# A graph-convolution layer with residual and layer norm: the norm moves into the residual's tile, row groups are formed two at a time from the fifth superrow, and the gather ring starts uncleared

## The chip, the cores and the metric

The kernel runs on one core of one Trainium2 chip. The metric is the device time of one execution in microseconds (us). TensorE is called PE here, VectorE DVE, ScalarE ACT, GpSimd POOL and SyncE SP; PEld is the loading of weights into PE.

## What is computed

Sizes: B = 8 batches, N = 4096 nodes, 256 features in and out, all float32. About two in a thousand entries of `adj` are set before it is made symmetric, with a heavy head: low node numbers have many neighbours.

```python
HW = einsum('bnf,fo->bno', x, W)
A_norm = relu((A + A.T) * 0.5)
D = sum(A_norm, axis=1)
d = where(D > 0, D ** -0.5, 0)
L = eye(N) - d[:, None] * A_norm * d[None, :]
y = relu(einsum('nm,bmo->bno', L, HW))
out = layernorm(x + y)            # over the last axis, eps 1e-5
```

## The kernel before

**Stage one** reads `adj` in blocks of 512 x 512. For superrow i (eight of them, 512 rows each) and j >= i, `symmetrise` (L310) transposes a block on PE, adds its partner on DVE (L318), takes relu and the half on ACT (L319), sums 64-wide pieces into `part` on DVE (L320), and stores the block to `a_dram` from ACT's queue (L326). `degrees(i)` (L333) follows each superrow: row sums, their power -0.5 on POOL (`r`), and four diagonal blocks stored to `a_dram` over the stored block.

In between, `form(m, known)` (L355) makes row group m of G = x W: 128 nodes with all eight batches, a tile of 128 x 2048. It loads `xin` over SP's queue, transposes it on PE (L364), copies it on ACT (L365), multiplies it on PE (L374), and scales by `r` on ACT (L383) into `gt`, which goes to `g_dram` (L387). Row groups 24 to 31 are formed first, while their `r` isn't known; they stay unscaled in `held`, and `release` (L391) scales and stores them at the end of the stage. A `credit` (L407) decides how many row groups are formed after each block: one for each pair of blocks. Row groups 21 to 23 are left for the end.

From superrow 0 on, POOL, PE and DVE also make lists of the 64-wide pieces of A that are not empty: `patterns`, `place`, `spread`, `index` and so on. The lists of a unit give the rows to be gathered for it.

**Stage two** works by units u (16 of them), each of two row groups of the output, 2u and 2u+1; "group i" below is one of these 32. For a tile t of a unit's list, `gather` (L519) fetches 128 weights' rows from `a_dram` into `ga` (L527), and the matching 128 rows of `g_dram` into one of the 13 tiles of `ring` (L536), both with POOL's indirect DMAs. PE multiplies tile by tile (L623) into eight PSUM banks, four for group 2u (tag b0) and four for 2u+1 (tag b1). A list entry beyond the end has index N, and `bounds_check` decides whether such a row is fetched or left as it was; row N of `g_dram` and `a_dram` is zero. The ring's tiles are set to zero before use (L514).

When a group's last tile is through, `finish` (L558) runs its end:
- `evict`: ACT moves the four banks to `y` with relu and scale (L449, 128 x 512 each).
- one step later `moments`: DVE adds the residual `xr` (L458), takes the statistics (L463, L465, L466). `residual` (L441) then loads the `xr` of group i+2.
- five steps after that `normalise`: POOL's power (L470), DVE's eight scalings (L472), and the store of `y` to `out` over SP's queue (L480).

Before a unit ends, `lists(u)` (L569) makes the lists of later units: a few matmuls into two PSUM banks of tag b0, and DVE's list steps (L155 to L287, and L244 among them), which must have read these banks before PE can write the next unit's b0 group. Pools set the buffers: `y` has three, `xr` two. Nothing else but these buffers, the data and the order on each engine's queue decides when an instruction runs; the order is fixed when the program is built, and each engine takes its instructions in that order.

Of the kernel before, what the change touches and what calls it, by code (L numbers as in the profile page):

```python
# [8 lines left out]
F32 = mybir.dt.float32  # L9
AF = mybir.ActivationFunctionType  # L10
ALU = mybir.AluOpType
# [29 lines left out]
def kernel(  # L41
# [23 lines left out]
    nc = tc.nc  # L65
    B, N, F = x.shape
    FO = w.shape[1]
    P = 128
    S = 512
    A = S // P  # L70
    NS = N // S
    NB = N // P
# [6 lines left out]
    RING = 13  # L79
# [18 lines left out]
    r = const.tile([P, NB], F32, name="r")  # L98
# [194 lines left out]
    with (  # L293
# [8 lines left out]
        def load_adj(i, j):  # L302
            t = apool.tile([P, A, S], F32, tag="adj", name=f"adj_{i}_{j}")
            nc.sync.dma_start(
                t,
                adj[i * S : (i + 1) * S, j * S : (j + 1) * S].rearrange("(a p) s -> p a s", p=P),
            )
            return t
# [44 lines left out]
        held = {}  # L353
# [36 lines left out]

        def release(m):  # L391
            g = held.pop(m)
            nc.scalar.mul(g, g, r[:, m : m + 1])
            nc.scalar.dma_start(g_dram[m * P : (m + 1) * P, :], g)


        known, early = [], list(range(NB - HOLD, NB))
        credit = 0.0
        for i in range(NS):
            diag = stat1.tile([P, A, P], F32, tag="diag", name=f"diag_{i}")  # L400
            for j in range(i, NS):
                tij = load_adj(i, j)
                tji = load_adj(j, i) if j > i else tij
                symmetrise(i, j, tij, tji)
                if j > i:
                    symmetrise(j, i, tji, tij)
                credit += 1.0 if j > i else 0.5  # L407
                while credit >= 1.0 and (known or early):
                    if known:
                        form(known.pop(0), True)  # L410
                    else:
                        form(early.pop(0), False)
                    credit -= 1.0
                credit = min(credit, 1.0)
            degrees(i)
            known += range(i * A, min((i + 1) * A, NB - HOLD))
            if i < 2:
                for u in (2 * i, 2 * i + 1):
                    patterns(u)
                    tot = psum.tile([P, NK * NB], F32, tag="ix", name=f"tot_{u}", bufs=2)  # L420
                    low = psum.tile([P, NK * NB], F32, tag="ix", name=f"low_{u}", bufs=2)
                    count(u, tot, low)
                    place(u, tot, low)
            elif i < 4:
                for u in (2 * i - 4, 2 * i - 3)[: 4 - i]:
                    pr = psum.tile([P, 2, NB], F32, tag="ix", name=f"pr_{u}", bufs=2)
                    count_rest(u, pr[:, 0], pr[:, 1])
                    place_rest(u, pr[:, 0], pr[:, 1])
            elif i < 6:
                u = i - 4  # L430
                spread(u)
                pl = psum.tile([P, 2, tiles[u]], F32, tag="ix", name=f"pl_{u}", bufs=2)
                collect(u, pl)
                index(u, pl)
        for m in sorted(held):
            release(m)
        for m in known:
            form(m, True)


    def residual(i, ypool):  # L441
        xr = ypool.tile([P, B, F], F32, tag="xr", name=f"xr_{i}", bufs=2)
        nc.scalar.dma_start(xr, x[:, i * P : (i + 1) * P, :].rearrange("b p f -> p b f"))
        return xr

    def evict(i, py, ypool):
        y = ypool.tile([P, B, FO], F32, tag="y", name=f"y_{i}", bufs=3)
        for c in range(G // S):
            nc.scalar.activation(  # L449
                y.rearrange("p b o -> p (b o)")[:, c * S : (c + 1) * S],  # L450
                py[c],
                AF.Relu,
                scale=minus_r[:, i : i + 1],
            )
        return y

    def moments(i, y, xr, stat):
        nc.vector.tensor_add(y, y, xr)  # L458
        stats = stat.tile([P, B, 6], F32, tag="stats", name=f"stats_{i}")
        mv = stat.tile([P, B, 2], F32, tag="mv", name=f"mv_{i}")  # L460
        rstd = stat.tile([P, B], F32, tag="rstd", name=f"rstd_{i}")
        for b in range(B):
            nc.vector.bn_stats(stats[:, b, :], y[:, b, :])  # L463
        for b in range(B):
            nc.vector.bn_aggr(mv[:, b, :], stats[:, b, :])  # L465
        nc.vector.tensor_scalar(rstd, mv[:, :, 1], EPS, None, ALU.add)  # L466
        return mv, rstd

    def normalise(i, y, mv, rstd):
        nc.gpsimd.tensor_tensor(rstd, rstd, neg_half[:, :B], ALU.pow)  # L470
        for b in range(B):
            nc.vector.tensor_scalar(  # L472
                y[:, b, :],
                y[:, b, :],
                mv[:, b, 0:1],
                rstd[:, b : b + 1],
                ALU.subtract,
                ALU.mult,
            )
        nc.sync.dma_start(out[:, i * P : (i + 1) * P, :].rearrange("b p f -> p b f"), y)  # L480

    a_rows = a_dram.rearrange("j (c q) -> (j c) q", q=P)
    a_pairs = a_dram.rearrange("j (c q) -> (j c) q", q=2 * P)
# [22 lines left out]
    with (  # L506
# [3 lines left out]
        tc.tile_pool(name="psum2", bufs=4, space=bass.MemoryType.PSUM) as psum,  # L510
    ):
        ring = [gath.tile([P, G], F32, tag=f"g{k}", name=f"g{k}", bufs=1) for k in range(RING)]
        for gt in ring:
            nc.vector.memset(gt, 0.0)  # L514
        steps = [(u, step) for u in range(NU) for step in steps_of(u)]
        order = [(u, k, t) for u, step in steps for k, t in step]
        got = {}
# [1 line left out]
        def gather(n):  # L519

            if n >= len(order):
                return
            u, kind, t = order[n]
            gi, ai = plan[u]
            both = len(targets(kind)) == 2
            at = gath.tile([P, 2 * P], F32, tag="a", name=f"ga_{u}_{t}")
            nc.gpsimd.indirect_dma_start(  # L527
                out=at if both else at[:, :P],
                out_offset=None,
                in_=a_pairs if both else a_rows,  # L530
                in_offset=bass.IndirectOffsetOnAxis(ap=ai[:, t : t + 1], axis=0),
            )


            gt = ring[n % RING]
            nc.gpsimd.indirect_dma_start(  # L536
                out=gt,
                out_offset=None,
                in_=g_dram,
                in_offset=bass.IndirectOffsetOnAxis(ap=gi[:, t : t + 1], axis=0),  # L540
                bounds_check=N - 1,
                oob_is_err=False,
            )
            got[u, t] = (at, gt)
# [3 lines left out]
        def after(n, fn, *args):  # L548
            later.append((n, fn, args))

        for n in range(RING):
            gather(n)
        n = RING
        xr = {i: residual(i, ypool) for i in range(2)}
        py = {}
        left = {}

        def finish(i):  # L558
            y = evict(i, py.pop(i), ypool)

            def rest():
                mv, rstd = moments(i, y, xr.pop(i), stat)
                if i + 2 < NB:
                    xr[i + 2] = residual(i + 2, ypool)
                after(5, normalise, i, y, mv, rstd)

            after(1, rest)

# [86 lines left out]
    with tc.If(short > 0):  # L655
        with (
            tc.tile_pool(name="full", bufs=3) as full,
            tc.tile_pool(name="ypool3", bufs=2) as ypool,
            tc.tile_pool(name="stat3", bufs=3) as stat,
            tc.tile_pool(name="psum3", bufs=8, space=bass.MemoryType.PSUM) as psum,  # L660
        ):
            for i in range(NB):
                lt = full.tile([P, NB, P], F32, tag="l", name=f"l_{i}", bufs=2)
                nc.sync.dma_start(
                    lt, a_dram[:N, i * P : (i + 1) * P].rearrange("(m p) q -> p m q", p=P)
                )
                py = [psum.tile([P, S], F32, tag="ps", name=f"pz_{i}_{c}") for c in range(G // S)]
                for m in range(NB):
                    gt = full.tile([P, G], F32, tag="g", name=f"gf_{i}_{m}", bufs=4)
                    nc.sync.dma_start(gt, g_dram[m * P : (m + 1) * P, :])  # L670
                    for c in range(G // S):
                        nc.tensor.matmul(
                            py[c],
                            lhsT=lt[:, m, :],
                            rhs=gt[:, c * S : (c + 1) * S],
                            start=(m == 0),
                            stop=(m == NB - 1),
                        )
                y = evict(i, py, ypool)
                mv, rstd = moments(i, y, residual(i, ypool), stat)  # L680
                normalise(i, y, mv, rstd)


# [26 lines left out]
```

## Time and profile before

| What | us |
|---|---|
| three runs | 1771.97, 1778.17, 1779.72 |
| median | 1778.17 |
| profiled execution | 1779.99 |
| its span, first to last instruction | 1778.2 |
| PE busy, of the span | 1521.4 (86%) |
| DVE busy | 823.4 (46%) |
| POOL busy | 804.5 (45%) |
| ACT busy | 368.7 (21%) |
| first matmul of stage two, after the start | 587.0 |

The page divides the span into 40 slices of 44 us. Of each it gives the busy tenths, here PE's, then the granted clock, then the share of the 16 DMA engines:

```profile
PE   6998686868866799999999999998979849679874
...
PEclk8999898989987899999999999999999979889988
DMA  9999999999977984797999999899998986877973
```

Stage one fills the first 13 slices and is full of DMA traffic; stage two begins in the 14th. A busy PE isn't PE at its peak, since matmuls overlap and their ends are modelled. Idle time of an engine that isn't the bottleneck costs nothing.

### The profile page before, as it was taken

What the parts mean: (1) busy time and instruction counts of PE and PEld (TensorE: products, weight loads), DVE (VectorE), ACT (ScalarE), POOL (GpSimd) and SP (SyncE); (2) the same over time, 40 slices, a digit from 0 to 9 for tenths busy, and PEclk for the clock granted to TensorE, in tenths of its full rate; (3) what the DMA queues carried; (4) which work ended last, traced back from release to release, by engine and by line L of the source; (5) the groups of instructions that cost most, each with busy time, mean ns of one, the idle gap of its engine ahead of it and who ended that gap; (6) DMA issues with size and microseconds to landing.
All of it is one profiled execution on the core that took longest, in us unless ns stands there. A gap on an engine that the chain in (4) does not pass through costs nothing.

```text
span 1778.2 us, 18495 instructions
## 1 busy us (share of the span) xinstructions
PE 1521.4 (86%) x6504; PEld 804.2 (45%) x6504; DVE 823.4 (46%) x1841; ACT 368.7 (21%) x457; POOL 804.5 (45%) x1079
## 2 busy tenths in 40 slices
PE   6998686868866799999999999998979849679874
PEld 5887575757755244343433333333333314224331
DVE  5686898656644000425154264346344245233134
ACT  3555443535545000101011001001000100000011
POOL 3000000000003453566767777678677764575641
PEclk8999898989987899999999999999999979889988
DMA  9999999999977984797999999899998986877973
GB/s 338 387 376 376 403 342 348 347 375 392 396 262 281 406 329 152 261 362 266 398 366 387 375 360 372 330 361 357 353 376 305 379 326 214 326 270 284 354 284 112
DMA packets 234547, 590.67 MB, mean 332 GB/s; under 512 B 19863, under 2 KB 122567, under 8 KB 194839
## 3 DMA queue, kind: packets, MB, share of 16 engines
q0 software_dynamic: 57456, 318.57, 46.5%
q1 hardware_dynamic: 100352, 134.23, 21.4%
q10 hardware_dynamic: 76640, 136.61, 20.7%
q8 instruction: 54, 0.88, 0.2%
q14 instruction: 45, 0.37, 0.1%
HBM read 494.47 MB, written 136.34 MB: 355 GB/s over the span
## 4 chain that ended last, share of the span: by engine, by line
PE 54%; DMA 19%; issue 12%; DVE 9%; ACT 3%; POOL 2%; ACTq 0%; POOLq 0%; SPq 0%; DVEq 0%
PE py L623 43%; DMA out_dram<-y 7%; PE pg L374 6%; DMA g<-g_dram,gi 5%; DMA adj<-in_adj_dram 5%; PE tr L315 3%; DVE sym L318 2%; DVE y L472 1%; DVE g L514 1%; ACT sym L319 1%; DVE part L320 1%; ACT xt L365 1%; POOL g L536 1%; POOL ga L527 1%; PE xtr L364 1%
## 5 line engine op out<-in xcount | busy, mean ns | idle before, releaser
L623 PE MATMUL py<-g,ga 128*64 128x512 f32 (+1 forms) x3368 | 1058.3, 601 | 108.8 <-ACT y L449 82.4
L623 PEld LDWEIGHTS py<-g,ga 128*64 128x64 f32 (+1 forms) x3368 | 400.7, 157 | 754.0 <-issue 647.4
L536 POOL DMA_INDIRECT g<-g_dram,gi x317 | 385.2, 1215 | 295.3 <-PE py L623 176.2
L527 POOL DMA_INDIRECT ga<-a_dram,ai x317 | 336.2, 1060 | 131.4 <-issue 84.9
L458 DVE TENSOR_TENSOR y<-y,xr 128x2048 f32<-128x2048 f32 x32 | 73.3, 2290 | 640.4 <-ACT y L449 640.4
L449 ACT ACTIVATE y<-py,minus_r 128x512 f32<-128x512 f32 x128 | 83.5, 688 | 1104.9 <-PE py L623 639.9
L374 PE MATMUL pg<-w_sb,xt 128*128 128x256 f32 x1024 | 253.9, 405 | 63.2 <-ACT xt L365 63.1
L374 PEld LDWEIGHTS pg<-w_sb,xt 128*128 128x128 f32 x1024 | 203.0, 203 | 107.2 <-ACT xt L365 77.8
L318 DVE TENSOR_TENSOR sym<-tr,adj 128x512 f32<-128x512 f32 x256 | 159.3, 683 | 125.3 <-PE tr L315 100.9
L340 POOL TENSOR_TENSOR r<-e,neg_half 128x4 f32<-128x4 f32 x8 | 8.1, 1012 | 402.4 <-DVE e L339 402.4
L315 PE MATMUL tr<-ident,adj 128*128 128x128 f32 x1024 | 132.3, 288 | 43.4 <-DMA adj<-in_adj_dram 26.7
L320 DVE TENSOR_REDUCE part<-sym 128x32 f32<-128x2048 f32 x64 | 144.2, 2277 | 19.6 <-ACT sym L319 19.6
L319 ACT ACTIVATE sym<-sym 128x2048 f32<-128x2048 f32 x64 | 122.4, 1912 | 142.6 <-DVE sym L318 104.7
L315 PEld LDWEIGHTS tr<-ident,adj 128*128 128x128 f32 x1024 | 123.1, 150 | 52.8 <-issue 23.1
L472 DVE TENSOR_SCALAR y<-y,mv,rstd 128x256 f32<-128x256 f32 x256 | 86.9, 412 | 89.3 <-POOL rstd L470 89.3
L463 DVE BATCH_NORM_STATS2 stats<-y 128x6 f32<-128x256 f32 x256 | 86.9, 410 | 0.6
L383 ACT ACTIVATE gt<-pg,r 128x512 f32<-128x512 f32 x96 | 66.0, 690 | 99.7 <-PE pg L374 77.4
L470 POOL TENSOR_TENSOR rstd<-rstd,neg_half 128x8 f32<-128x8 f32 x32 | 53.5, 1673 | 48.0 <-DVE rstd L466 47.3
L364 PE MATMUL xtr<-ident,xin 128*128 128x128 f32 x512 | 67.3, 283 | 9.0 <-ACT gt L383 6.0
L365 ACT COPY xt<-xtr 128x512 f32<-128x512 f32 x128 | 68.9, 582 | 15.6 <-PE xtr L364 9.1
L244 DVE TENSOR_TENSOR hot<-iota_q,at 128x4096 bf16<-128x4096 f32 x16 | 70.6, 4415 | 0.0
L364 PEld LDWEIGHTS xtr<-ident,xin 128*128 128x128 f32 x512 | 59.9, 146 | 13.1 <-ACT gt L383 6.8
(92 smaller groups left out, 380.6 us busy)
## 6 DMA issues: line engine op xcount, KB each, us to landing
adj<-in_adj_dram SPq DMA_DIRECT2D x64, 1024.0 KB, 11.9
a_dram<-sym ACTq DMA_DIRECT2D x64, 1024.0 KB, 10.0
xin<-in_x_dram SPq DMA_DIRECT2D x32, 1024.0 KB, 15.6
xr<-in_x_dram ACTq DMA_DIRECT2D x32, 1024.0 KB, 15.4
out_dram<-y SPq DMA_DIRECT2D x32, 1024.0 KB, 18.8
g_dram<-gt ACTq DMA_DIRECT2D x24, 1024.0 KB, 7.2
g_dram<-held ACTq DMA_DIRECT2D x8, 1024.0 KB, 9.1
ga<-a_dram,ai POOLq DMA_INDIRECT x317, 8.0
```

The costliest lines, as they stand in the source:

```text
L315: nc.tensor.transpose(pt[:, c * P : (c + 1) * P], tji[:, c, a * P : (a + 1) * P], ident)
L318: nc.vector.tensor_add(sym[:, a, :], pt, tij[:, a, :])
L319: nc.scalar.activation(sym, sym, AF.Relu, scale=0.5)
L320: nc.vector.tensor_reduce(part[:, i * A : (i + 1) * A, j * S // Q : (j + 1) * S // Q], sym.rearrange("p a (c q) -> p a c q", q=Q), AX.X, A ...
L364: nc.tensor.transpose(pt[:, k, c, :], xin[:, b + k, c * P : (c + 1) * P], ident)
L365: nc.scalar.copy(xt[:, b : b + 2], pt)
L374: nc.tensor.matmul(pg[:, k * FO : (k + 1) * FO], lhsT=xt[:, b + k, c, :], rhs=w_sb[:, c, :], start=(c == 0), stop=(c == FC - 1),)
L463: nc.vector.bn_stats(stats[:, b, :], y[:, b, :])
L472: nc.vector.tensor_scalar(y[:, b, :], y[:, b, :], mv[:, b, 0:1], rstd[:, b : b + 1], ALU.subtract, ALU.mult,)
L527: nc.gpsimd.indirect_dma_start(out=at if both else at[:, :P], out_offset=None, in_=a_pairs if both else a_rows, in_offset=bass.IndirectOff ...
L536: nc.gpsimd.indirect_dma_start(out=gt, out_offset=None, in_=g_dram, in_offset=bass.IndirectOffsetOnAxis(ap=gi[:, t : t + 1], axis=0), boun ...
L623: nc.tensor.matmul(py[2 * u + b][c][rows, :], lhsT=at[:, off + rows.start : off + rows.stop], rhs=gt[:, c * S : (c + 1) * S], start=new_ro ...
```

## The change

- The addition's result is written into the residual's tile, called `z` in the new code. Statistics, scaling and the store work on it. `y` holds the evicted group only until the addition has read it. `xr` gets three buffers in place of two, `y` two in place of three.
- The load of the residual goes over SP's queue, not ACT's. It is issued for group i+3 after the store of group i, and no longer for i+2 after the addition of i. Since it takes the tile that group i leaves, it waits for that store.
- From superrow 4 on (the fifth), the credit of a block is doubled, so that two row groups may be formed after a pair.
- Held row groups are released after the superrow that they belong to: 24 to 27 after superrow 6, 28 to 31 after superrow 7. Of these the odd ones are scaled on DVE.
- The ring is not set to zero. The first 13 gathers fetch the zero row N for entries beyond the end, in place of leaving the tile as it is.

```diff
@@ -390,8 +390,12 @@
         def release(m):
             g = held.pop(m)
-            nc.scalar.mul(g, g, r[:, m : m + 1])
+            if m % 2:
+                nc.vector.tensor_scalar(g, g, r[:, m : m + 1], None, ALU.mult)
+            else:
+                nc.scalar.mul(g, g, r[:, m : m + 1])
             nc.scalar.dma_start(g_dram[m * P : (m + 1) * P, :], g)
+
         known, early = [], list(range(NB - HOLD, NB))
@@ -404,7 +408,7 @@
                 symmetrise(i, j, tij, tji)
                 if j > i:
                     symmetrise(j, i, tji, tij)
-                credit += 1.0 if j > i else 0.5
+                credit += (1.0 if j > i else 0.5) * (1 if i < 4 else 2)
                 while credit >= 1.0 and (known or early):
                     if known:
                         form(known.pop(0), True)
@@ -413,6 +417,9 @@
                     credit -= 1.0
                 credit = min(credit, 1.0)
             degrees(i)
+            for m in range(i * A, (i + 1) * A):
+                if m in held:
+                    release(m)
             known += range(i * A, min((i + 1) * A, NB - HOLD))
             if i < 2:
                 for u in (2 * i, 2 * i + 1):
@@ -432,19 +439,17 @@
                 pl = psum.tile([P, 2, tiles[u]], F32, tag="ix", name=f"pl_{u}", bufs=2)
                 collect(u, pl)
                 index(u, pl)
-        for m in sorted(held):
-            release(m)
         for m in known:
             form(m, True)
     def residual(i, ypool):
-        xr = ypool.tile([P, B, F], F32, tag="xr", name=f"xr_{i}", bufs=2)
-        nc.scalar.dma_start(xr, x[:, i * P : (i + 1) * P, :].rearrange("b p f -> p b f"))
+        xr = ypool.tile([P, B, F], F32, tag="xr", name=f"xr_{i}", bufs=3)
+        nc.sync.dma_start(xr, x[:, i * P : (i + 1) * P, :].rearrange("b p f -> p b f"))
         return xr
     def evict(i, py, ypool):
-        y = ypool.tile([P, B, FO], F32, tag="y", name=f"y_{i}", bufs=3)
+        y = ypool.tile([P, B, FO], F32, tag="y", name=f"y_{i}", bufs=2)
         for c in range(G // S):
             nc.scalar.activation(
                 y.rearrange("p b o -> p (b o)")[:, c * S : (c + 1) * S],
@@ -454,30 +459,31 @@
             )
         return y
-    def moments(i, y, xr, stat):
-        nc.vector.tensor_add(y, y, xr)
+    def moments(i, y, z, stat):
+
+        nc.vector.tensor_add(z, z, y)
         stats = stat.tile([P, B, 6], F32, tag="stats", name=f"stats_{i}")
         mv = stat.tile([P, B, 2], F32, tag="mv", name=f"mv_{i}")
         rstd = stat.tile([P, B], F32, tag="rstd", name=f"rstd_{i}")
         for b in range(B):
-            nc.vector.bn_stats(stats[:, b, :], y[:, b, :])
+            nc.vector.bn_stats(stats[:, b, :], z[:, b, :])
         for b in range(B):
             nc.vector.bn_aggr(mv[:, b, :], stats[:, b, :])
         nc.vector.tensor_scalar(rstd, mv[:, :, 1], EPS, None, ALU.add)
         return mv, rstd
-    def normalise(i, y, mv, rstd):
+    def normalise(i, z, mv, rstd):
         nc.gpsimd.tensor_tensor(rstd, rstd, neg_half[:, :B], ALU.pow)
         for b in range(B):
             nc.vector.tensor_scalar(
-                y[:, b, :],
-                y[:, b, :],
+                z[:, b, :],
+                z[:, b, :],
                 mv[:, b, 0:1],
                 rstd[:, b : b + 1],
                 ALU.subtract,
                 ALU.mult,
             )
-        nc.sync.dma_start(out[:, i * P : (i + 1) * P, :].rearrange("b p f -> p b f"), y)
+        nc.sync.dma_start(out[:, i * P : (i + 1) * P, :].rearrange("b p f -> p b f"), z)
     a_rows = a_dram.rearrange("j (c q) -> (j c) q", q=P)
     a_pairs = a_dram.rearrange("j (c q) -> (j c) q", q=2 * P)
@@ -510,8 +516,6 @@
         tc.tile_pool(name="psum2", bufs=4, space=bass.MemoryType.PSUM) as psum,
     ):
         ring = [gath.tile([P, G], F32, tag=f"g{k}", name=f"g{k}", bufs=1) for k in range(RING)]
-        for gt in ring:
-            nc.vector.memset(gt, 0.0)
         steps = [(u, step) for u in range(NU) for step in steps_of(u)]
         order = [(u, k, t) for u, step in steps for k, t in step]
         got = {}
@@ -538,7 +542,7 @@
                 out_offset=None,
                 in_=g_dram,
                 in_offset=bass.IndirectOffsetOnAxis(ap=gi[:, t : t + 1], axis=0),
-                bounds_check=N - 1,
+                bounds_check=N if n < RING else N - 1,
                 oob_is_err=False,
             )
             got[u, t] = (at, gt)
@@ -551,7 +555,7 @@
         for n in range(RING):
             gather(n)
         n = RING
-        xr = {i: residual(i, ypool) for i in range(2)}
+        xr = {i: residual(i, ypool) for i in range(3)}
         py = {}
         left = {}
@@ -559,10 +563,15 @@
             y = evict(i, py.pop(i), ypool)
             def rest():
-                mv, rstd = moments(i, y, xr.pop(i), stat)
-                if i + 2 < NB:
-                    xr[i + 2] = residual(i + 2, ypool)
-                after(5, normalise, i, y, mv, rstd)
+                z = xr.pop(i)
+                mv, rstd = moments(i, y, z, stat)
+
+                def end():
+                    normalise(i, z, mv, rstd)
+                    if i + 3 < NB:
+                        xr[i + 3] = residual(i + 3, ypool)
+
+                after(5, end)
             after(1, rest)
@@ -677,8 +686,9 @@
                             stop=(m == NB - 1),
                         )
                 y = evict(i, py, ypool)
-                mv, rstd = moments(i, y, residual(i, ypool), stat)
-                normalise(i, y, mv, rstd)
+                z = residual(i, ypool)
+                mv, rstd = moments(i, y, z, stat)
+                normalise(i, z, mv, rstd)
 # ---- launch: one core; inputs and outputs as the reference has them ----
```

## The prediction

> **What bounds the kernel now.** I read the chain that ended last, then the engines' busy time by stage, then the waits of the second stage, then one turn of the repeating pattern in the timeline, and last the transfers' landing times. The chain first, from the page:
>
> ```profile
> PE 54%; DMA 19%; issue 12%; DVE 9%; ACT 3%; POOL 2%; ACTq 0%; POOLq 0%; SPq 0%; DVEq 0%
> PE py L623 43%; DMA out_dram<-y 7%; PE pg L374 6%; DMA g<-g_dram,gi 5%; DMA adj<-in_adj_dram 5%; PE tr L315 3%; DVE sym L318 2%; DVE y L472 1%; DVE g L514 1%; ACT sym L319 1%; DVE part L320 1%; ACT xt L365 1%; POOL g L536 1%; POOL ga L527 1%; PE xtr L364 1%
> ```
>
> The output transfers stand on it with 7%: a store that nobody should need to wait for. Busy time by stage (us; PE, PEld, DVE, ACT, POOL, then clock, DMA share, GB/s):
>
> ```profile
> 900.00:1300.00 400.00, 391.38 (x1587) 146.44 (x1583) 190.50 (x563) 31.91 (x48) 302.30 (x253) 0.99 0.97 362
> 1300.00:1450.00 150.00, 123.47 (x463) 46.86 (x461) 57.86 (x170) 9.91 (x16) 113.47 (x99) 0.93 0.95 358
> 1450.00:1600.00 150.00, 108.01 (x391) 43.56 (x392) 54.31 (x160) 11.43 (x18) 81.70 (x68) 0.85 0.73 268
> ```
>
> Up to 1300 PE is fed; after it both PE and DMA have holes. Who makes the holes, in the waits from 600 on (engine, line, waited for: total us, times, longest):
>
> ```profile
> ACT y L449 <- DMA out_dram<-y: 438.2, 15, 43.1
> ...
> PE py L623 <- ACT y L449: 82.4, 7, 23.6
> ```
>
> Evictions wait for stores of three groups earlier (three y buffers), and PE waits for the evictions. One turn in the timeline (start, duration):
>
> ```profile
> 1387.44 2.42 ACT L449 ACTIVATE y<-py,minus_r 128x512 f32<-128x512 f32 x4 [34.60 <-DMA out_dram<-y]
> ...
> 1389.89 2.29 DVE L458 TENSOR_TENSOR y<-y,xr 128x2048 f32<-128x2048 f32 x1 [13.81 <-ACT y L449]
> 1392.10 2.67 DVE L472 TENSOR_SCALAR y<-y,mv,rstd 128x256 f32<-128x256 f32 x8
> ...
> 1394.83 0.37 SPq L480 DMA_DIRECT2D out_dram<-y  x1
> ...
> 1418.11 2.42 ACT L449 ACTIVATE y<-py,minus_r 128x512 f32<-128x512 f32 x4 [28.25 <-DMA out_dram<-y]
> ...
> 1420.56 2.29 DVE L458 TENSOR_TENSOR y<-y,xr 128x2048 f32<-128x2048 f32 x1 [22.43 <-ACT y L449]
> ...
> 1432.75 4.42 DVE L244 TENSOR_TENSOR hot<-iota_q,at 128x4096 bf16<-128x4096 f32 x1
> ...
> 1438.26 2.75 DVE L472 TENSOR_SCALAR y<-y,mv,rstd 128x256 f32<-128x256 f32 x8
> ```
>
> This is a loop: evict 19, add 19, normalise 17, store 17 lands after 23 us, evict 20, add 20, list work, normalise 18 (done at 1441.0), and so on. DVE takes its instructions in order, and normalise i stands behind add i+2. From add 12 (1148.2) to add 26 (1628.7) a pair of groups takes 480.5 / 7 = 68.6 us.
>
> What a 1 MB transfer takes to land, in 900 to 1300 (last column, median us):
>
> ```profile
> xr<-in_x_dram ACTq DMA_DIRECT2D x12, 1024.0 KB, 20.6
> out_dram<-y SPq DMA_DIRECT2D x11, 1024.0 KB, 19.9
> ```
>
> and in 1300 to 1778:
>
> ```profile
> out_dram<-y SPq DMA_DIRECT2D x17, 1024.0 KB, 17.1
> xr<-in_x_dram ACTq DMA_DIRECT2D x13, 1024.0 KB, 7.5
> ```
>
> A lone one takes about 6 (the last store: 5.1): the rest is the gathers' traffic.
>
> **What the Trainium skill says.** "DMA: Bandwidth & Descriptors", section "Queues, rings and completion order": each DMA engine goes round its queues packet by packet. The landings of 5.1 to 25.1 us for equal stores agree. The same page, "Issuing engines are not separate DMA queues": all issuers end on the same 16 engines, so another issuer saves only issue time; here that is 0.37 us. The same page, "Two DMAs through the same engine are not ordered": a dependent transfer needs its issuer to wait for the first one's semaphore. Hence SP must sit until a store has landed before it may reload that tile; the kernel before has no such pair, so its trace cannot show it. "Perfetto Trace Analysis", "Identifying the Most-Contended Engine": busy matmul time is a poor measure, which is why I go by waits.
>
> **The second stage, part by part.** The group's life moves from y (three buffers) into z, the residual's tile (also three). Evictions now wait only for the addition of two groups earlier: the 438 us of ACT's wait and PE's 82 go. What is late next is the addition. z of group i is reloaded only after store i-3 has landed, so the path is: normalise i-3, store, land, load, land, add i. Before, the load started right after add i-2 and was there in time. The load is thus moved from beside the loop into the loop.
>
> Where does this bind? In the trace of before, the time from issuing store i-3 to add i is 36 us for i=9, 34 (10), 15 (11), 32 (12), 20 (13), 37 (14), 10 (15), 32 (16). The new path needs 19.9 + 20.6 + 0.4 = 41. So it binds from about group 10.
>
> What queues behind the wait: SP now alternates store i, load i+3 (waits for store i), store i+1. In the instruction order of the two builds DVE is nearly the same in this stage, but late normalise 2u and 2u+1 stand together ahead of additions 2u+3 and 2u+4. Behind a waiting add on DVE stand the list steps and the next normalise; the lists of a unit must be read before PE gets two of its four banks for the next unit.
>
> A pair therefore costs: add to the end of the normalise behind the lists, 1420.6 to 1441.0 = 20.4; store 2u; store 2u+1 (SP was held by the wait); load of 2u+4; three issues, 1.2. Load 2u+3 runs beside store 2u+1.
> - Busy rows: 20.4 + 1.2 + 2 x 19.9 + 20.6 = 82.
> - Late rows: 20.4 + 1.2 + 2 x 17.1 + 7.5 = 63.3.
>
> Which holds? Gathers of a late unit are 16 tiles of 1.05 MB and some 0.1 MB of weights, with stores and loads 22 to 23 MB, at 380 GB/s 59 us. They start when PE gets its banks, about 8 us after the add, so the engines are full until some 67 us after it. The first store (22) and the second (19) fall in that time; the last load, at 63, gets the engines nearly alone: 6 to 8. Sum 20.4 + 1.2 + 41 + 8 = 71. I take P = 71, ends 63 and 82.
>
> Start of the loop: stage one ends 8 us earlier (below), so store 7 is issued at 1038.5, lands 1058.4, z of 10 lands 1079.4; add 10 to the end of normalise 8 is 15.1 (1094.5); store 8 to 1114.4; store 9 to 1135; load 12 to 1156. Add 12 is at 1156, before 1148.2. Then seven pairs; the last two units' pairs have no lists, 11 us less each, and the seventh 2 less; from add 30 to add 31 pass 8.5 (statistics and normalise 28), a store of 12 and a load of 8, with issues 29; add 31 to the end as before, 17.5 (1760.7 to 1778.2). Span = 1156 + 7P - 2 + 2(P - 11) + 29 + 17.5 = 1178.5 + 9P. With 71: 1817.5. Break-even is P = 66.6.
>
> **The first stage.** Chain there (start, duration):
>
> ```profile
> 543.38 10.21 DMA g_dram<-held
> ...
> 579.86 1.78 DVE g L514
> ...
> 587.04 53.37 PE py L623 x129
> ```
>
> The 13 memsets (13 x 1.76 = 23 us of DVE) go, at no gain alone: the first gather waited until 577.2 for the last g_dram store and landed 10 us later. Row blocks 20 to 23 and four of eight releases move ahead of the last block of A. That block's transposes stood at 509.4. Four row groups cost PE 9 us each (1.9 transposes, 7.1 matmul), 36, less some 12 of PE holes since 390: about 534. From there: transposes to the A store's issue 5.1, landing 10.9, four diagonal stores 1.9, a release 2 (the other two now on DVE; bound by the normalise rate of 2.7), four 1 MB stores 11, then address and data gather 2.3 and 10 to the first matmul: 43 to 45. So 578 against 587: 8 to 9 us gained, I take 8; bounds 0 (PE without holes) and 20 (4 row groups wholly in DMA time). Loads of x from SP instead of ACT: nothing at the start, they come before any need.
>
> **Rivals.**
> - Faster: the loads and second stores fall into pauses of the gathers, as the late rows' 7.5 us has it. P = 63 gives 1745; with 20 us from stage one 1733. For it: PE and DMA both have holes after 1450, and 438 us of waits go. Against: ending PE's waits packs the gathers, and transfers beside them take 20. It decides below P = 66.6.
> - Even: P between 65.7 and 67.6, the load's cost paid by stage one and shorter evictions: about 1778.
> - Much slower: all four transfers in gather traffic, SP's queue served in order, P = 79: 1890. Against: DMA has 59 us of work in such a period, so the last ones are alone.
> - Stage one not shorter at all: 8 more, 1825; part of the forecast's range.
>
> **How the numbers follow.** The profiled execution took 1779.99 with a span of 1778.2, the median of the runs is 1778.17: no correction. Forecast 1817, own range 1770 to 1875 (P 66 to 77), chance 0.6; much slower 0.1; even 0.1; faster 0.2. What a measurement here can tell from no change is about 0.5%, 9 us. Slower 0.7, within 0.1, faster 0.2. The range leaves out a tenth on each side: 1742 to 1880.
>
> **What would show it.** Right: ACT's wait for the store gone; DVE's additions waiting for the load (DMA xr) in most late groups; 69 to 74 us per pair from add 12 on; PE's holes between units, ended by DVE's list steps; the first matmul near 579. Wrong: additions waiting for ACT or PE, pairs below 66 us, or loads landing in 6 us throughout.

## The result: 1823.3 us after 1775.1, and the profile after the change

| | before | after |
|---|---|---|
| median of 4 runs each, on one chip | 1775.07 | 1823.30 |
| lowest and highest | 1769.81, 1779.72 | 1819.01, 1829.88 |
| profiled execution (span) | 1779.99 (1778.2) | 1829.88 (1828.2) |

The ratio is 1.0276, with a 95% interval of 1.0226 to 1.0325: slower. The experiments below were measured in three series, each beside the kernel before. In the second the whole change lost again, but less (1.0173, with 1.0092 to 1.0254). In the first the kernel before itself took 1833 us in place of 1775, for a reason that stays open; so ratios are formed within a series only. They compare each kernel's fast runs (within 1.5% of its fastest), while the times given are medians of all its runs.

The chain of work that ended last (followed back from the last instruction, at each step to what released it), from the page of the kernel after:

```profile
DMA 37%; PE 33%; DVE 14%; issue 12%; ACT 2%; POOL 1%; ACTq 0%; SPq 0%; DVEq 0%; POOLq 0%
PE py L632 24%; DMA out_dram<-xr 22%; DMA xr<-in_x_dram 7%; PE pg L374 6%; DMA adj<-in_adj_dram 4%; DVE xr L478 2%; DVE sym L318 2%; PE tr L315 2%; DVE hot L244 2%; DVE stats L469 2%; DMA a_dram<-sym 2%; DVE xr L464 2%; ACT sym L319 1%; DMA g<-g_dram,gi 1%; DVE part L320 1%
```

Before, PE's multiplications of stage two held 43% of the chain and the output's stores 7%. Now PE holds 24%, the stores 22%, and the load of the residual, which was not among the chain's larger parts before, 7%. Busy time by stage (us; PE, PEld, DVE, ACT, POOL, then clock, DMA share, GB/s):

```profile
900.00:1300.00 400.00, 357.65 (x1461) 135.46 (x1458) 169.43 (x500) 32.34 (x48) 283.45 (x245) 0.94 0.92 345
1300.00:1450.00 150.00, 133.16 (x496) 50.13 (x496) 58.70 (x173) 11.36 (x17) 96.73 (x83) 0.92 0.84 310
```

In 900 to 1300 PE was busy for 391 of 400 us; now for 358. The stretch that was full has got holes. Who makes them, from the waits of stage two (from 600 on; engine, line, waited for: total us, times, longest):

```profile
DVE xr L464 <- DMA xr<-in_x_dram: 450.0, 22, 43.1
...
PE py L632 <- DVE pos_k L159: 94.6, 7, 28.1
...
ACT y L454 <- DVE xr L464: 52.2, 4, 15.6
```

The evictions' wait for a store (438 us before) is gone from the list. In its place the addition waits for the load of its residual, 22 times, 450 us in all. PE's holes between units are now ended by DVE's list steps, which stand behind that addition. One turn in the timeline (start, duration), with the instructions of DVE, PE and SP's queue that make the loop; the additions are those of groups 18, 19 and 20:

```profile
1408.57 2.29 DVE L464 TENSOR_TENSOR xr<-xr,y 128x2048 f32<-128x2048 f32 x1 [7.73 <-DMA xr<-in_x_dram]
...
1416.36 45.46 PE L632 MATMUL py<-g,ga 128*64 128x512 f32 x156 [14.00 <-DVE pos_k L159]
...
1424.30 2.67 DVE L478 TENSOR_SCALAR xr<-xr,mv,rstd 128x256 f32<-128x256 f32 x8
...
1427.01 0.38 SPq L486 DMA_DIRECT2D out_dram<-xr  x1
...
1429.55 2.67 DVE L478 TENSOR_SCALAR xr<-xr,mv,rstd 128x256 f32<-128x256 f32 x8
...
1443.61 0.37 SPq L448 DMA_DIRECT2D xr<-in_x_dram  x1
...
1444.03 0.57 SPq L486 DMA_DIRECT2D out_dram<-xr  x1
...
1464.55 2.29 DVE L464 TENSOR_TENSOR xr<-xr,y 128x2048 f32<-128x2048 f32 x1 [32.34 <-DMA xr<-in_x_dram]
...
1467.08 0.37 SPq L448 DMA_DIRECT2D xr<-in_x_dram  x1
...
1473.13 2.29 DVE L464 TENSOR_TENSOR xr<-xr,y 128x2048 f32<-128x2048 f32 x1 [2.79 <-DMA xr<-in_x_dram]
```

Read it from addition 18 at 1408.57. PE gets its banks 7.8 us later (1416.36). Normalise 16 and 17 are done at 1427.0 and 1432.2. Store 16 is issued at once. Store 17 is not: SP's next instruction is load 19, which waits until store 16 has landed (1443.6), so store 17 goes out at 1444.0, 11.8 us after its data were ready. It lands at 1467.1, and only then load 20 starts. One turn of the loop takes in a pair of groups, and the turn from addition 18 to addition 20 is 18.4 (to the end of normalise 16) + 16.6 (store 16) + 0.4 + 23.1 (store 17) + 6.0 (load 20) = 64.5 us.

This is one of the shorter turns. The seven from addition 12 to 26 take 59 to 88 us; by SP's issues and the additions' starts their parts are:

| us | shortest | mean | longest |
|---|---|---|---|
| addition 2u+2 to store 2u | 7.8 | 17.4 | 20.7 |
| store 2u lands | 15.0 | 16.8 | 19.3 |
| store 2u+1 lands | 17.5 | 27.1 | 41.5 |
| load 2u+4 issued to its addition | 5.9 | 9.4 | 23.0 |

With 0.4 between the first landing and the issue of the second store, the means make 71.1. SP's waits for stores, from 900 on:

```profile
SPq L448 <- DMA out_dram<-xr: 561.3, 27, 40.9
```

The landings in 900 to 1300, from the DMA view of the kernel after (last column: median us):

```profile
xr<-in_x_dram SPq DMA_DIRECT2D x10, 1024.0 KB, 22.7
out_dram<-xr SPq DMA_DIRECT2D x10, 1024.0 KB, 22.4
```

and from 1300 to the end:

```profile
out_dram<-xr SPq DMA_DIRECT2D x19, 1024.0 KB, 18.0
xr<-in_x_dram SPq DMA_DIRECT2D x17, 1024.0 KB, 8.1
```

Before, the stores took 19.9 and 17.1 and the loads 20.6 and 7.5. So the medians are 10 to 13% higher in the first stretch and 5 to 8% in the second. Single stores did take longer: up to 41.5 us here, 25.1 before (and up to 41.1 in `e_y4`, the fastest kernel below). The main difference is that the additions now wait for a store and a load in a row.

Where the 50 us between the two profiled executions come from, by place:

| | before | after | change since the line above |
|---|---|---|---|
| first matmul of stage two | 587.0 | 601.3 | +14.3 |
| addition 12 | 1148.2 | 1183.6 | +21.1 |
| addition 26 (seven pairs later) | 1628.7 | 1681.1 | +17.0 |
| end | 1778.2 | 1828.2 | -2.4 |

### The profile page after: what moved, and what is told of

It reads as the page before. It is cut to its first block, busy times and chain, and to the rows that moved or that the text cites. A ratio compares the mean times of both kernels' runs of the same rounds, so it can differ in the third digit from the quotient of the medians.

```text
span 1828.2 us, 18422 instructions
## 1 busy us (share of the span) xinstructions
PE 1514.8 (83%) x6504; PEld 801.0 (44%) x6504; DVE 803.9 (44%) x1832; ACT 363.0 (20%) x453; POOL 791.7 (43%) x1079
## 4 chain that ended last, share of the span: by engine, by line
DMA 37%; PE 33%; DVE 14%; issue 12%; ACT 2%; POOL 1%; ACTq 0%; SPq 0%; DVEq 0%; POOLq 0%
PE py L632 24%; DMA out_dram<-xr 22%; DMA xr<-in_x_dram 7%; PE pg L374 6%; DMA adj<-in_adj_dram 4%; DVE xr L478 2%; DVE sym L318 2%; PE tr L315 2%; DVE hot L244 2%; DVE stats L469 2%; DMA a_dram<-sym 2%; DVE xr L464 2%; ACT sym L319 1%; DMA g<-g_dram,gi 1%; DVE part L320 1%
## 5 line engine op out<-in xcount | busy, mean ns | idle before, releaser
L632 PE MATMUL py<-g,ga 128*64 128x512 f32 (+1 forms) x3368 | 1054.3, 608 | 156.8 <-DVE pos_k L159 94.6
L540 POOL DMA_INDIRECT g<-g_dram,gi x317 | 377.1, 1190 | 222.3 <-PE py L632 124.0
L464 DVE TENSOR_TENSOR xr<-xr,y 128x2048 f32<-128x2048 f32 x32 | 73.3, 2291 | 714.5 <-DMA xr<-in_x_dram 450.0
L531 POOL DMA_INDIRECT ga<-a_dram,ai x317 | 331.4, 1045 | 119.4 <-issue 84.1
L340 POOL TENSOR_TENSOR r<-e,neg_half 128x4 f32<-128x4 f32 x8 | 8.1, 1012 | 461.5 <-DVE e L339 461.5
L478 DVE TENSOR_SCALAR xr<-xr,mv,rstd 128x256 f32<-128x256 f32 x256 | 86.5, 412 | 89.0 <-POOL rstd L476 89.0
L469 DVE BATCH_NORM_STATS2 stats<-xr 128x6 f32<-128x256 f32 x256 | 87.0, 412 | 0.8
L365 ACT COPY xt<-xtr 128x512 f32<-128x512 f32 x128 | 68.8, 582 | 16.3 <-DMA adj<-in_adj_dram 7.5
```

The lines of the kernel that those rows point to most:

```text
L464: nc.vector.tensor_add(z, z, y)
L469: nc.vector.bn_stats(stats[:, b, :], z[:, b, :])
L478: nc.vector.tensor_scalar(z[:, b, :], z[:, b, :], mv[:, b, 0:1], rstd[:, b : b + 1], ALU.subtract, ALU.mult,)
L531: nc.gpsimd.indirect_dma_start(out=at if both else at[:, :P], out_offset=None, in_=a_pairs if both else a_rows, in_offset=bass.IndirectOff ...
L540: nc.gpsimd.indirect_dma_start(out=gt, out_offset=None, in_=g_dram, in_offset=bass.IndirectOffsetOnAxis(ap=gi[:, t : t + 1], axis=0), boun ...
L632: nc.tensor.matmul(py[2 * u + b][c][rows, :], lhsT=at[:, off + rows.start : off + rows.stop], rhs=gt[:, c * S : (c + 1) * S], start=new_ro ...
```

## The experiments

**First series: one stage alone.** `e_s1` is the kernel before with only stage one changed, `e_s2` the kernel after with stage one as it was. `e_s2z4` gives `e_s2` a fourth z tile, and `e_actload` issues the residual's load from ACT's queue in the kernel after.

```diff
# e_s1, against the kernel before
-            nc.scalar.mul(g, g, r[:, m : m + 1])
+            if m % 2:
+                nc.vector.tensor_scalar(g, g, r[:, m : m + 1], None, ALU.mult)
+            else:
+                nc.scalar.mul(g, g, r[:, m : m + 1])
...
-                credit += 1.0 if j > i else 0.5
+                credit += (1.0 if j > i else 0.5) * (1 if i < 4 else 2)
...
+            for m in range(i * A, (i + 1) * A):
+                if m in held:
+                    release(m)
...
-        for m in sorted(held):
-            release(m)
```

> Only the first stage's part of the change on the kernel before (two row groups a pair from superrow 4, releases after their superrow, the odd ones on DVE); ring cleared, y and xr as before. In the trace of the changed kernel the first matmul of stage two came at 601.3, 14 later than before. Theory (the tail after the last block is laid bare, and stage two can't win it back, since PE is fed without a hole up to 1236): first matmul near 601, time 1775 + 14 = 1789, ratio 1.008 (1.004 to 1.012). Rival (the loop's pauses in stage two absorb the late start): first matmul near 601, time 1775, ratio below 1.003. Rival two (the late start came from the second stage's loads or from the uncleared ring): first matmul at 587 or earlier.

Measured: 1836.0 us against 1833.5 in its series, ratio 1.0027 (0.9999 to 1.0056), first matmul at 594.9. Stage one by itself gains nothing; of the loss of 0.8% that was expected there is no sign either.

```diff
# e_s2, against the kernel after: stage one as before
...
-                credit += (1.0 if j > i else 0.5) * (1 if i < 4 else 2)
+                credit += 1.0 if j > i else 0.5
...
-            for m in range(i * A, (i + 1) * A):
-                if m in held:
-                    release(m)
...
+        for m in sorted(held):
+            release(m)
```

> The change without its first-stage part: stage one as before, z in the residual's tile, loads on SP's queue, ring not cleared. Theory (the load in the loop costs some 36 of the 50 us): first matmul 585 to 588, additions waiting for the load by 400 us or more, time 1800 to 1815, ratio 1.015 to 1.022. Rival (stage one makes the whole loss, since the loop only binds after a late start): below 1785. Rival two (stage one's late start is absorbed): 1823, as the whole change.

Measured: 1810.5, ratio 0.9886 (0.9823 to 0.9950). The time is in the forecast range, yet by the ratio this kernel is faster, because the kernel before was some 58 us above its usual time in this series. So the loss is shown only against a kernel before at its usual time, and the experiment was repeated. The first matmul came at 591.9, only 3 us ahead of `e_s1`'s; in this series the late start was that small.

```diff
# e_s2z4, against e_s2 (room: the zeros come from part, two fewer ga tiles)
...
-        xr = ypool.tile([P, B, F], F32, tag="xr", name=f"xr_{i}", bufs=3)
+        xr = ypool.tile([P, B, F], F32, tag="xr", name=f"xr_{i}", bufs=4)
...
-        xr = {i: residual(i, ypool) for i in range(3)}
+        xr = {i: residual(i, ypool) for i in range(4)}
...
-                        xr[i + 3] = residual(i + 3, ypool)
+                        xr[i + 4] = residual(i + 4, ypool)
```

> e_s2 with four z tiles in place of three (reload for group i+4; 13 weight buffers in place of 15 and the zero row in another tile's memory, to make room). Addition 2u+4 then waits for one store and one load after normalise 2u, 20.4 + 0.8 + 20 + 8 to 20 = 49 to 61 us per pair, at or below the 59 us of DMA work. Theory: the waits of additions for the load nearly vanish (below 100 us), a pair takes 60 to 65 us after group 12, time 1700 to 1745, ratio 0.957 to 0.983. Rival (the loss comes from y's two buffers or from more DMA traffic at once): as e_s2, 1800 or more.

Measured: 1764.0, ratio 0.9607 (0.9542 to 0.9671), 46 us less than `e_s2` in the same series. One more tile between a store and the reload of its tile saves time, as it must if the loop through these tiles is what binds, and `y` still has two tiles here. But it saves less than was expected (1700 to 1745): the additions still wait 222 us for loads, where under 100 was forecast. The reason is seen at `e_z4`.

```diff
# e_actload, against the kernel after
-        nc.sync.dma_start(xr, x[:, i * P : (i + 1) * P, :].rearrange("b p f -> p b f"))
+        nc.scalar.dma_start(xr, x[:, i * P : (i + 1) * P, :].rearrange("b p f -> p b f"))
```

> The whole change, but the residual loads on ACT's queue in place of SP's; tile and waits else the same. Store 2u+1 is then no longer held until store 2u has landed, but ACT stands until store i has landed, and in its order evictions stand behind. Theory (the held store costs 10 to 19 us of a pair of 71): a pair at 58 to 66 if evictions are in time, time 1720 to 1790; if ACT's stand holds PE up in turn, 1800 to 1830 with PE waiting for evictions. Rival (SP's order costs nothing, contention alone does): 1823, and PE not waiting for evictions.

Measured: 1806.5, ratio 0.9856 (0.9792 to 0.9920), against a kernel before that was out of its usual time; also repeated. A pair takes 67.7 us, not 58 to 66.

**Second series: again, and where a spare tile helps.** Both kernels were run once more as they are.

> The kernel before, for a trace on the same chip as the others of this call: ratio 1. If before takes about 1833, the trace tells which stage the extra 55 us are in. Theory: stage two, in evictions that wait for stores (438 us in the first trace, then more), with the first matmul within 8 us of 587. Rival: stage one, or PE's granted clock, throughout.

Measured: 1775.2 against 1777.3, ratio 0.9987 (0.9969 to 1.0005): the kernel before is at its usual time again.

> The whole change again, because the kernel before took 1833 us on the chip of the last four runs and 1775 on the first one: is the loss of 2.8% the same there? Theory (the load in the loop lengthens a fixed chain): 1.02 to 1.03 times before, on any chip. Rival (what before loses on a chip where its stores land later or its evictions wait longer, the change has already lost: evictions no longer wait for stores): 0.99 to 1.01 where before takes 1820 or more, 1.02 to 1.03 where it takes under 1785.

Measured: 1806.1, ratio 1.0173 (1.0092 to 1.0254). The loss is there, the time some 17 us less than in the first result. The additions wait 394 us for loads, the first matmul comes at 601.2, addition 12 at 1185.0, and a pair takes 68.3 us. So these two traces agree in the start to some 1.5 us and differ in the pairs.

`e_z4` is the edit of `e_s2z4` on the kernel after.

> The whole change with four z tiles (13 weight buffers, zero row in another tile's memory), as e_s2z4 but with the changed first stage. Theory: the first stage's part costs what it did in e_s1 against before (0.3%) to 14 us, so 1764 + 5 to 14 = 1769 to 1778 where e_s2z4 takes 1764. Rival (the changed first stage helps once the loop isn't bound by stores): below 1760.

Measured: 1761.2 (the median of 15 runs from 1743 to 1776), ratio 0.9854 (0.9825 to 0.9882), 45 us less than `r_after` in the same series. The forecast of 1769 to 1778 was too high. Its waits from 600 on:

```profile
DVE xr L464 <- DMA xr<-in_x_dram: 289.3, 15, 35.4
...
PE py L632 <- DVE pos_k L159: 55.0, 3, 27.3
```

A fourth tile loosens the loop but doesn't open it: the load still can't start before a store has landed, and 289 us of waiting remain.

`e_y4` asks what the same room brings in the kernel before: a fourth `y`, the normalised group staying in `y` as before, with the load beside the loop. Here too the room comes from `part` and two `ga` tiles, and the ring isn't cleared.

```diff
# e_y4, against the kernel before
-    zero = const.tile([NB, P], F32, name="zero")
+    zero = part.rearrange("p m s -> p (m s)")[:NB, :P]
...
-        y = ypool.tile([P, B, FO], F32, tag="y", name=f"y_{i}", bufs=3)
+        y = ypool.tile([P, B, FO], F32, tag="y", name=f"y_{i}", bufs=4)
...
-        tc.tile_pool(name="gath", bufs=RING + 2) as gath,
+        tc.tile_pool(name="gath", bufs=RING) as gath,
...
-        for gt in ring:
-            nc.vector.memset(gt, 0.0)
...
-                bounds_check=N - 1,
+                bounds_check=N if n < RING else N - 1,
```

> The kernel before with four y buffers in place of three, ring not cleared (13 weight buffers, zero row in another tile's memory): the other way to spend 8 KB on the same wait. Eviction i waits for store i-4. Theory: a pair's chain loses one of its two stores, ACT's wait for stores falls from 438 us to under 150, time 3 to 5% below before, as e_s2z4 or better, since the loads stay beside the loop. Rival (a fourth tile does nothing since DVE's order is the bound): within 1% of before.

Measured: 1711.2, ratio 0.9631 (0.9584 to 0.9678): faster than both kernels, as forecast. Its waits from 600 on, and its busy time by stage:

```profile
ACT y L449 <- DMA out_dram<-y: 87.6, 4, 32.7
```

```profile
1300.00:1450.00 150.00, 140.56 (x495) 54.40 (x495) 60.15 (x178) 10.99 (x16) 110.22 (x93) 1.00 0.95 355
1450.00:1600.00 150.00, 144.97 (x553) 57.75 (x553) 71.66 (x218) 16.50 (x24) 117.27 (x97) 0.98 0.95 358
```

The evictions' wait for stores is 88 us, where it was 438, and PE is busy for 286 of these 300 us, against 231 before. A pair takes 59.6 us from addition 12 to 26. Its transfers, from 1300 to the end:

```profile
out_dram<-y SPq DMA_DIRECT2D x17, 1024.0 KB, 24.0
xr<-in_x_dram ACTq DMA_DIRECT2D x12, 1024.0 KB, 22.8
```

Both are slower to land than those of the kernel after (18.0 and 8.1) in a kernel that is 95 us shorter than `r_after`. So a transfer's own length matters less than whether the next group must wait for its landing.

**Third series: one part alone, repeated where the kernel before ran at its usual time.** `r_s1`, `r_s2` and `r_act` are `e_s1`, `e_s2` and `e_actload`.

> The first stage's part alone again: in its first run the kernel before took 1833 us in the same call, 55 more than in the two others, so a small loss could hide. Theory: first matmul at 595 to 601, 8 to 14 later than before; PE is fed up to 1236 in before, so it stays: ratio 1.004 to 1.010. Rival: absorbed by the pauses after 1300, ratio below 1.003.

Measured: 1778.2 against 1774.1, ratio 1.0023 (1.0006 to 1.0040). The forecast of a loss of 0.4% to 1% missed; stage one costs some 4 us (1 to 7 by the interval). And yet its first matmul comes at 599.9:

```profile
599.92 2.79 PE L627 MATMUL py<-g,ga 128*64 128x512 f32 x3 [41.55 <-DVE g L518]
```

This is 13 to 14 us later than in the kernel before (587.0, in `r_before` 585.5). By the medians most of a late start is made up before the end. Where and by what isn't shown: the evictions' wait for stores is no shorter (473.8 us, and 474.4 in `r_before`), and the two traces can't be set side by side, since the profiled execution of `r_s1` was the longest of its 19 and that of `r_before` the second shortest of its 20.

> The second stage's part alone (and the uncleared ring) again, for the same reason. Theory (the load in the loop costs some 20 to 36 us whatever stage one does): first matmul at 587, addition 12 some 25 to 30 later than in before, ratio 1.010 to 1.020. Rival (the loop binds only after the late start of the changed stage one): ratio below 1.005.

Measured: 1799.7 (four runs from 1788 to 1815, the longest one profiled), ratio 1.0138 (1.0078 to 1.0198). With the old stage one its first matmul is at 585.5, and the wait is there in full:

```profile
DVE xr L460 <- DMA xr<-in_x_dram: 456.6, 23, 41.9
```

So most of the loss, 1.4% of the 1.7% to 2.8%, is stage two's, and it needs no help from stage one. Addition 12, at 1164.0, is 16 us later than in the kernel before, where 25 to 30 was forecast.

> The whole change with the loads on ACT's queue, again beside a kernel before of known speed. Theory (the store that SP holds costs some of the chain): addition 2u+4's wait for its load shorter, a pair 64 to 68 us, ratio 0.99 to 1.01. Rival (SP's order is of no weight, or ACT's stand gives it all back): ratio 1.017 to 1.028, as the whole change.

Measured: 1794.8, ratio 1.0134 (1.0095 to 1.0173), 68.8 us a pair. `r_after`, in another series, had 1.0173 (1.0092 to 1.0254): the intervals overlap, so what SP's order costs isn't settled. The waits of `r_act` from 600 on:

```profile
ACT y L454 <- DMA out_dram<-xr: 413.9, 8, 58.1
DVE xr L464 <- DMA xr<-in_x_dram: 391.6, 18, 44.5
```

The load no longer holds the next store, and SP waits for no landing any more. Now ACT stands until the store has landed, ahead of the next eviction. Most of this is time in which ACT would have waited for PE anyway: that wait is 514 us here and 1021 in `r_after`, and PE's multiplications wait 0.5 us for evictions. But the additions wait for their loads as long as in `r_after` (394 us). From 1300 on a load now takes 22.5 us to land, in the median, where the kernel after had 8.1. Probably the loads now run beside the next store, which no longer waits for them to be issued; this wasn't tested.

`e_y4rel` adds to `e_y4` only the release of held row groups after their superrow, the odd ones on DVE. The credit stays single.

> e_y4 with the changed release (after its superrow, odd ones on DVE), but one row group a pair as before, so that row groups 20 to 23 stay behind the last block. Theory (what made the start late was that the last block came after the row groups, so its tail had no cover; the release itself is early work): first matmul at 575 to 587, time 1700 to 1712, ratio 0.957 to 0.963. Rival (the early release delays the last block's stores): first matmul after 590, ratio above 0.966.

Measured: 1707.7, ratio 0.9642 (0.9606 to 0.9678), and the first matmul:

```profile
583.93 6.64 PE L625 MATMUL py<-g,ga 128*64 128x512 f32 x13 [16.25 <-issue]
```

It is 3 us earlier than `e_y4`'s 587.0. The early release by itself thus doesn't make the start late; what remains of stage one's edits is the doubled forming, alone or together with the release. The ratio is just above the forecast 0.957 to 0.963, and that of `e_y4` within the intervals.

## Why the prediction was right, and which of its terms were wrong

**Direction and cause: right; the closeness of the total is luck.** The load moved into the loop normalise, store, land, load, land, add. The wait named there is the first of the two traces' differences (450 us for 438), `r_s2` has it with the old stage one, a fourth tile reduces it to 289 us and takes 45 us off, and the opposite use of the same room (`e_y4`) takes 66 us off the kernel before. That `y` has only two tiles isn't what binds: the evictions of the kernel after wait 52 us for additions, and PE waits for no eviction. The total came within 6 us because a start that was 22 us later than worked out and an end that was 17 us shorter nearly cancel, as shown below.

**The pair's 71 us: right in sum, not in its parts.** From addition 12 to 26 pass 497.5 us, 71.07 a pair. But `r_after` had 68.3, under the 69 to 74 that were named as a sign, and the prediction's 20.4, 22, 19 and 8 are 17.4, 16.8, 27.1 and 9.4 in the mean of the seven turns. The first store was put 5 us too high and the second 8 too low; `r_after` and `r_s2` have the same order (second store 25.8 and 29.0). So the agreement to a tenth is luck. Confirmed one by one: store 2u+1 is held on SP behind the load (11.8 us); PE gets its banks about 8 us after the addition (7.8); the last load lands in about 6 us in five of the seven turns; the list steps end PE's holes (94.6 us).

**Stage one 8 us earlier: wrong, it is 14 us later.** The term that failed is "36, less some 12 of PE holes since 390: about 534". The last block's transposes stand at 557.05. The 36 us of four row groups were right: from 300 to these transposes PE is busy for 166.0 us before (to 509.4) and 201.4 after (to 557.05), 35.4 more. But its idle time there didn't fall by 12; it rose by 12, from 43.4 to 55.7. PE's waits in that stretch, before:

```profile
PE pg L374 <- ACT xt L365: 27.8, 22, 12.5
...
PE tr L315 <- DVE sym L318: 3.9, 1, 3.9
```

and after:

```profile
PE pg L374 <- ACT xt L365: 35.9, 17, 11.0
PE tr L315 <- DVE sym L318: 19.4, 6, 4.4
```

One such place, at the start of a superrow, in the timeline after:

```profile
509.78 1.01 POOL L340 TENSOR_TENSOR r<-e,neg_half 128x4 f32<-128x4 f32 x1 [47.76 <-DVE e L339]
...
512.67 1.14 DVE L346 SCALAR_TENSOR_TENSOR diag<-ident,minus_e,diag 128x128 f32<-128x128 f32 x4
513.05 2.75 ACTq L349 DMA_DIRECT2D a_dram<-diag  x4
515.85 1.91 ACT L319 ACTIVATE sym<-sym 128x2048 f32<-128x2048 f32 x1 [8.15 <-issue]
...
517.66 0.57 ACT L365 COPY xt<-xtr 128x512 f32<-128x512 f32 x1
...
518.28 8.35 PE L374 MATMUL pg<-w_sb,xt 128*128 128x256 f32 x24 [6.55 <-ACT xt L365]
```

The row group formed there needs ACT's copies of `xt`. In ACT's queue these stand behind the four diagonal stores of the superrow before, and the stores wait for DVE's `diag` steps (L346), which need POOL's power (L340) and DVE's sums of the whole superrow. The chain at 461.5 is the same. The holes at the last two superrow starts are 6.2 us (at 461.5) and 6.5 (518.3), where they were 3.9 and 3.0 before; that of 11.0 at 391 was there before with 12.5. PE's wait for DVE's sums grew more; one of its six waits, of 4.4 us, ended at 300.6 and began ahead of the stretch; before, its like ended at 297.8 and isn't counted. The other waits fell from 12.7 to 3.9 us. What delayed DVE was not followed further. The prediction counted the moved row groups' PE time, and not the queues of ACT and DVE that they pass through. From the transposes on it was right: 44.3 us to the first matmul (43 to 45 predicted).

**Addition 12 at 1156: 27.6 late.** 22.3 of it is the first matmul's error (601.3 for 579); 5.3 remain. `r_s2`, whose stage one has no change, has addition 12 at 1164.0, which is 1156 plus the 8 us that the prediction had taken off for stage one. The sum comes out, its steps don't: addition 10 was due at 1079.4 + 8 = 1087.4 and came at 1098.5, and from there to addition 12 passed 65.5 us, not 76.6.

**The end: shorter than worked out.** The last two pairs took 109.0 us, where 60 + 60 - 2 = 118 was summed, and additions 30 to 31 took 20.6, not 29. The end in the timeline after:

```profile
1774.92 0.37 SPq L448 DMA_DIRECT2D xr<-in_x_dram  x1
1775.34 0.57 SPq L486 DMA_DIRECT2D out_dram<-xr  x1
1784.02 0.37 SPq L448 DMA_DIRECT2D xr<-in_x_dram  x1
1797.71 2.96 SPq L486 DMA_DIRECT2D out_dram<-xr  x2
1802.57 0.38 SPq L448 DMA_DIRECT2D xr<-in_x_dram  x1
```

The load at 1784.02 shows that the store issued at 1775.34 had landed: 8.7 us, where 19 was assumed. The load at 1802.57 follows a store of 4.9 us, where 12 was assumed. The last gather was issued at 1767.4. These 9.0 and 8.4 us, against the 27.6 of addition 12 and 0.5 of the seven pairs, leave +10.7: 1828.2 for a predicted 1817.5.

**Parts costed at nothing.** The ring's clearing: `e_y4`, without it, begins stage two at 587.0 as the kernel before does. Right. The releases on DVE, bounded by 2.7 us each, take 1.28, ACT's 2.0. The bound was taken from eight scalings of 256 elements. The Trainium skill has a closer price, in "VectorE: DVE Perf Modes", section "The perf-mode tier table (the rule you actually need)": 1.227 us for a float32 tensor_scalar of 2048 elements in SBUF. This trace agrees to some 4%. The rival of a faster kernel, with transfers that fall into pauses, was decided by the pair: 71.1, over the break-even of 66.6, and PE's busy share of 900 to 1300 fell. The even rival fell with it, and so did the much slower one, with its 79 us. The rival that stage one gains nothing was nearer than the forecast: it loses 14 us of start.

Not tried: the doubled credit without the early release, either of them alone in the kernel before with its three `y` tiles, and three `y` tiles in the kernel after. Why the kernel before took 1833 us in the first series stays open. `e_s1`, which has the old stage two, shows only where such time lies: addition 12 is 19 us later than in `r_s1`, and a pair takes 71.7 us, not 67.5.

## What to carry to other kernels

A tile that is loaded, worked on in place and stored puts store, landing, load and landing in one loop: count this loop per buffer before moving a result into its input's tile, and spend spare room where it keeps a load out of the loop (a fourth `y` took 3.7% off the kernel before; a fourth z left the changed one only 1.5% below it). For a reload that waits for a store, look at what stands behind it on the issuer's queue, but don't count on another queue: here the additions waited as long for their loads there. When work is moved earlier, walk every engine's queue that it passes through, not only the engine that bounds it.

## What the hardware showed that was not expected

- Equal stores of 1 MB took 4.8 to 41.5 us to land in one execution of the kernel after (25.1 at most before). The 4.8 came after the last gather.
- A load took 8.1 us in the median, from 1300 on, when it waited on the same queue until a store was through, and 22.5 when it was issued from another queue (`r_act`).
- A start that was 13 to 14 us late in the trace went with 4 us at the end by the medians (`r_s1`). What takes up the rest isn't shown.
